# The last expert group's results: scattered to their tokens tile by tile instead of fetched by gathers

## The chip, the cores and the metric

The kernel runs on one core of a Trainium2 chip. The metric is the device time of one execution in microseconds (us); the kernel before takes 1362.29 us (median of three runs, 1362.22 to 1365.09).

## The reference

A "macaron" block over 4 sequences of 512 tokens with 128 features, all in float32. The input passes six residual stages; only the last one, a mixture of experts (MoE), is touched by the change:

```python
x = x + 0.5 * _L0_ffn_ref(_layernorm(x), ...)
x = x + _L0_attn_ref(_layernorm(x), ...)          # a state-space (mamba) scan
x = x + 0.5 * _L0_ffn_ref(_layernorm(x), ...)
x = x + 0.5 * _L1_ffn_ref(_layernorm(x), ...)     # MoE
x = x + _L1_attn_ref(_layernorm(x), ...)
x = x + 0.5 * _L1_ffn_ref(_layernorm(x), ...)     # MoE, the same weights
```

```python
rw = _route(x, gate_w, gate_bias)     # per token 8 of 64 experts, with weights; 0 elsewhere
expert_out = vmap(lambda gw, uw, dw: silu(x @ gw.T) * (x @ uw.T) @ dw.T)(Wg, Wu, Wd)   # 64 experts, 88 wide
routed = einsum('eth,te->th', expert_out, rw)
out = routed + shared                 # shared: one dense expert, 176 wide
```

The kernel computes for each token only its 8 chosen experts.

## The kernel before, in words

The engines are PE (TensorE), DVE (VectorE), ACT (ScalarE), POOL (GpSimd) and SP, which only issues DMAs. POOL issues the indirect DMAs, 128 rows each.

**The planner.** The program records every operation, with the tiles it reads and writes, into a `Plan`. `schedule` then orders each engine's queue by a model of costs (`costs`), data dependencies, free buffers and a rank (`rank(...)` sets one for each engine), and `issue` emits the operations in that order. Each engine works through its queue strictly in order. Line 558 is the call in `issue` that emits most operations, so most rows of the profile have that line and are told apart by their tiles. An `Op` with an `apart` name is a write to rows that no other write of that name touches, so that these writes do not wait for each other; `past` makes an operation wait for all writes of a name. Between two such writes POOL does a small memset (`scratch`, line 627).

**The MoE layer.** It runs twice. Each time the four sequences form two groups of two sequences (`GROUPS`), so there are four groups, g = 0 to 3; `LAST` in the changed kernel is g = 3. A group has 1024 tokens with 8 experts each, that is 8192 rows.

- `send` (line 1065) routes one sequence and works out for each token and each of its 8 experts the row in the DRAM tensor `sent` that this pair gets. Rows of one expert are contiguous and padded to whole tiles of 128 rows. `at` holds the row numbers as integers and `top` as floats, both with one added before and taken off after. `xt` is the normalized input, token by token (128 partitions, 4 tiles of tokens). 32 scatters per sequence (4 tiles x 8 experts, `scatter`, line 1147) write the rows.
- `by_tiles` (line 1165) runs the experts on 96 tiles (`OFTEN`), in 24 batches of four tiles. `batch` (line 1170) loads four tiles with one DMA (`xr`, three buffers), transposes them on PE (`xc`), multiplies with the expert's gate and up weights, applies silu and the product (`hr`), transposes (`hc`) and multiplies with the down weights; ACT copies the result out of PSUM (`yr`) and SP writes it to the DRAM tensor `back`, in the same row order as `sent`. A row is addressed as partition times 128 (`most`) plus the tile's number. PE reads the number of each tile's expert into registers. If a group needs more than 96 tiles, a branch (`rest`, line 1248) does the others; every engine passes that branch, and on the path that skips it the queue waits for its DMAs. `nothing` and `zero` clear `sent` and part of `back` at the start (`clear`), so that padded rows hold zeros.
- `take` (line 1291) fetches the results of one sequence: for each tile of 128 tokens 8 gathers (`gather`, line 1156, on POOL, from `back` by `at`) into tiles `y` (16 buffers), and DVE adds them up with the routing weights `by` into `total` (one product and seven `scalar_tensor_tensor`). In the second layer each tile of tokens is then transposed on PE, added to x on DVE and written to the output by SP.

**The order at the end.** `work` (line 1454) is `by_tiles` and then `take` for both sequences. A group is worked on after the next one has been sent. So POOL's queue ends with: the sends of g = 3, the 64 gathers of g = 2 (after the branch of g = 2, beside the experts of g = 3), and the 64 gathers of g = 3 (after the branch of g = 3).

Of the kernel before, what the change touches and what calls it, by code (L numbers as in the profile page):

```python
# [24 lines left out]
F32 = mybir.dt.float32  # L27
U32 = mybir.dt.uint32
I32 = mybir.dt.int32
AF = mybir.ActivationFunctionType  # L30
ALU = mybir.AluOpType
AX = mybir.AxisListType
PSUM = bass.MemoryType.PSUM

P = 128
NB, S, D = 4, 512, 128
NT = S // P
# [14 lines left out]
MOST = {n: ((n * S * TOPK + E * (P - 1)) // P + 3) // 4 * 4 for n in (1, 2)}  # L52
OFTEN = {2: 96, 1: 72}
INDIRECT = 1.25
READ = 4
PART = 11

# [221 lines left out]
class Plan:  # L279
# [100 lines left out]
    def costs(self, op):  # L380
# [36 lines left out]
        if op.name in ("scatter", "gather"):  # L417
            return INDIRECT, INDIRECT + 6.0
        if op.eng == "gpsimd":
# [153 lines left out]
def macaron(ctx: ExitStack, tc: tile.TileContext, a: dict, out: bass.AP):  # L573
# [50 lines left out]
    numbers = fixed.tile([P, 1], F32, tag="numbers", name="numbers")  # L624
    real.gpsimd.iota(numbers, pattern=[[0, 1]], base=0, channel_multiplier=1, allow_small_or_imprecise_dtypes=True)
    scratch = fixed.tile([1, 8], F32, tag="scratch", name="scratch")
    plan.between = lambda: real.gpsimd.memset(scratch, 0.0)
# [41 lines left out]
    most = MOST[2]  # L669
    sent, backs = ([dram.tile([most * P, D], f"{n}{i}", bufs=1) for i in range(k)] for n, k in (("sent", 3), ("back", 2)))  # L670
    rank(0, 0, 0, 15)
    nothing = stage.tile([P, 2 * D], "nothing", bufs=1)
    nc.gpsimd.memset(nothing, 0.0)
    zero = dram.tile([P * 8 * D], "zero", bufs=1)
    for i in range(4):
        nc.sync.dma_start(out=zero.rearrange("(p x) -> p x", p=P)[:, i * 2 * D : (i + 1) * 2 * D], in_=nothing)
    chunks = []
    for rows in sent:
        to = rows.rearrange("(n p i) d -> n p (i d)", n=most // 8, i=16)
        chunks += [(to[n], zero.rearrange("(p x) -> p x", x=16 * D)) for n in range(most // 8)]  # L680
    for rows in backs:
        to = rows.rearrange("(p i) d -> p (i d)", p=P)
        for i in range(min(OFTEN.values()), most, 8):
            chunks.append((to[:, i * D : (i + 8) * D], zero.rearrange("(p x) -> p x", p=P)))
    chunks = iter(chunks)
# [350 lines left out]
    def count(b, prior):  # L1036
# [19 lines left out]

        xt = slots.tile([P, NT, D], "xt", bufs=2, fifo=True)
        ps = aux()
        plan.hold(xt)
        for t in range(NT):  # L1060
            nc.tensor.transpose(ps[:, t * P : (t + 1) * P], xn[:, t * P : (t + 1) * P], ident)
        nc.scalar.copy(xt.rearrange("p t d -> p (t d)"), ps)
        return xn, m8, sc, ranks, xt

    def send(g, b, before_):
# [4 lines left out]
        with plan.turn("route"):  # L1070
# [42 lines left out]
            for t in range(NT):  # L1113
                nc.vector.max(top[:, t, :], at_row[:, t, :])
                nc.vector.tensor_scalar_add(at[:, t], top[:, t], -1.0)

            with ranked(0.6, 5.7 if g < 2 and b else 1.6, 1, 5, g):
# [8 lines left out]
        for t in range(NT):  # L1126
            for k in range(TOPK):
                scatter(rows, at[:, t, k : k + 1], xt[:, t], g)
        return dict(ranks=ranks, held=held, base=base, end=end, mine=mine, taken=taken, fetch=(at, by), xn=xn, rows=rows)
# [16 lines left out]

    def scatter(rows, at, x, g):
        def go():
            return real.gpsimd.indirect_dma_start(  # L1149
                out=rows.real(), out_offset=bass.IndirectOffsetOnAxis(ap=at.real(), axis=0),  # L1150
                in_=x.real(), in_offset=None,
            )

        plan.call("gpsimd", "scatter", go, [rows], [at, x], f"sent{g}")

# [9 lines left out]
    def by_tiles(g, rows, of, taken, tiles, often):  # L1165

        back = backs[g % 2]
        firsts, lasts = firsts_of, lasts_of.rearrange("p e d -> p (e d)")

        def batch(nc, tiles_of, first, x, bank, xt, hs, ht, y, product, experts_, hold):  # L1170
            some = slice(first, first + 4)
            loads = nc.sync.dma_start(out=x, in_=tiles_of(rows)[:, some])
            experts_()
            ps = bank()
            hold(xt)
            for j in range(4):
                nc.tensor.transpose(ps[:, j * P : (j + 1) * P], x[:, j], ident)
            nc.vector.tensor_copy(xt, ps)
            for j in range(0, 4, 2):
                ps = bank()  # L1180
# [19 lines left out]
            nc.scalar.copy(y.rearrange("p i d -> p (i d)"), ps)  # L1200
            nc.sync.dma_start(out=tiles_of(back)[:, some], in_=y)
            return loads

        def tiles_of(x):
            return x.rearrange("(p i) d -> p i d", p=P)

        def buffers():
            return (
                bpool.tile([P, 4, D], "xr", bufs=3, fifo=True),
                bpool.tile([P, 4 * P], "xc", fifo=True),  # L1210
                bpool.tile([P, 4, I], "hr", fifo=True),
                bpool.tile([P, 4 * P], "hc", fifo=True)[0:I],
                bpool.tile([P, 4, D], "yr", fifo=True),
            )

# [10 lines left out]
        for first in range(0, often, 4):  # L1226
# [3 lines left out]
            def product(ps, lhs, w, n, j, to=to, held=held):  # L1230
# [6 lines left out]

            x, *others = buffers()
            batch(
                nc, tiles_of, first, x, lambda: banks.tile([P, S], "bank"), *others, product,  # L1240
                lambda: plan.call("tensor", "registers", partial(read, to, first), [held], [of]), plan.hold,
            ).past = f"sent{g}"


        x, *others = buffers()
        bank = banks.tile([P, S], "bank")

        def rest(past):
# [3 lines left out]
            )  # L1252
            x_, bank_, rows_, back_, *others_ = (v.real() for v in (x, bank, rows, back, *others))
            with tc.If(needed > often, preferred_fallthrough_block=False, name="rest"):
                for first in range(often, tiles, 4):
                    to = {}

                    def product(ps, lhs, w, n, j, to=to):
# [4 lines left out]
                    load = batch(  # L1263
                        real, lambda v: tiles_of({rows: rows_, back: back_}[v]), first, x_, lambda: bank_, *others_,
                        product, lambda: read(to, first), lambda *_: None,
                    )
                    past(load)

        plan.hold(x, bank, *others)
        plan.call("tensor", "branch", rest, [back], [rows, of, taken, firsts, lasts]).past = f"sent{g}"  # L1270
# [19 lines left out]

    def take(b, back, at, by, to=None):

        total = tpool.tile([P, NT, D], "total", bufs=1, fifo=True)
        for t in range(NT):
            y = [tpool.tile([P, D], "y", bufs=2 * TOPK, fifo=True) for _ in range(TOPK)]
            for k in range(TOPK):
                gather(y[k], back, at[:, t, k : k + 1])
            nc.vector.tensor_scalar_mul(total[:, t], y[0], by[:, t, 0:1])
# [155 lines left out]
    def work(g, blocks, rows, of, taken, fetch):  # L1454
        rank(12 + g if g < len(GROUPS[0]) else 19 + g, 2, 2, 6 + g, g)
        back = by_tiles(g, rows, of, taken, MOST[len(blocks)], OFTEN[len(blocks)])
        for b, f in zip(blocks, fetch):
            rank(0.4, 1.5, 1.5, 6, g + 0.5)
            take(b, back, *f, to=out[:, b * S : (b + 1) * S] if g >= len(GROUPS[0]) else None)

# [92 lines left out]
```

## Time and profile before

| | us |
|---|---|
| median of three runs | 1362.29 |
| the profiled execution | 1361.67 |
| its span, first to last instruction | 1359.9 |
| PE busy | 1151.3 (85%) |
| DVE busy | 983.2 (72%) |
| ACT busy | 638.9 (47%) |
| POOL busy | 557.0 (41%) |
| 256 scatters of `sent` on POOL | 282.2, 1.102 each |
| 256 gathers of `y` on POOL | 245.8, 0.960 each |
| scatters of g = 3, second sequence | from 1116.48 to 1158.18 |
| last copy of g = 2's results on ACT | 1163.34 |
| gathers of g = 2 | from 1168.94 to 1249.85 |
| last copy of g = 3's results on ACT | 1267.53 |
| gathers of g = 3 | from 1272.18 to 1351.80 |
| last addition to x on DVE | 1354.29 |

The profile is of one execution. A group of instructions is written as line, engine, operation, out<-in, with count, busy time and mean duration, then the idle time of that engine just before them and what ended it. "issue" means that the engine waited for nothing that the profile shows. In tables by stage the columns are the stretch (from:to and length), then for each engine its busy time and its number of instructions, then the clock granted to TensorE, the share of time that the DMA engines were busy, and GB/s. In the timeline a line is start, duration, engine, line, operation, and in brackets the idle time before it with what ended it. The chain that ended last is a list of start, duration and what the time went to.

### The profile page before, as it was taken

The page shows a single profiled execution, that of the slowest core. Times are in us where ns is not written, and L with a number is a line of the kernel's source. Part 1 is how long each engine was busy: PE and PEld are TensorE (multiplying, and loading weights), DVE is VectorE, ACT ScalarE, POOL GpSimd, SP SyncE. Part 2 cuts the span into 40 slices and gives each one's busy share as a digit, 9 for nine tenths or more (in the row PEclk, how much of TensorE's full clock was granted, in tenths as well). Part 3 has the DMA queues.
Part 4 walks back from the last instruction along what each step waited for, and adds up shares of the span by engine and source line. Part 5 has one row for each costly group of instructions (what it writes and reads, how often), then busy time and mean ns, then how long its engine had stood idle before and what let it go on. Part 6 is the DMA issues. An engine that isn't in the chain of part 4 may idle for free. (4 is left out here: it accounts for less than half of the span.)

```text
span 1359.9 us, 17468 instructions
## 1 busy us (share of the span) xinstructions
PE 1151.3 (85%) x5006; PEld 704.2 (52%) x5006; DVE 983.2 (72%) x2425; ACT 638.9 (47%) x1207; POOL 557.0 (41%) x794
## 2 busy tenths in 40 slices
PE   6999998999999978999789979999899889778200
PEld 4853332333343423579688645555556669778200
DVE  2168798999999895779477568988869688476222
ACT  4775866687755335343235535435353544222100
POOL 0000000000018593556677177380816418575475
PEclk8999998999999988999899989999999999898655
DMA  5074794755512208346466111010111136565221
GB/s 172 23 266 155 264 282 131 227 154 178 133 36 68 59 28 277 107 155 199 159 200 177 53 54 53 24 51 3 53 34 59 59 107 204 166 196 152 78 60 49
DMA packets 76313, 166.74 MB, mean 123 GB/s; under 512 B 17880, under 2 KB 30193, under 8 KB 75089
## 3 DMA queue, kind: packets, MB, share of 16 engines
q1 hardware_dynamic: 59825, 131.89, 30.9%
q0 software_dynamic: 16384, 33.59, 8.2%
q8 instruction: 50, 0.82, 0.2%
q14 instruction: 54, 0.44, 0.1%
HBM read 117.44 MB, written 83.36 MB: 148 GB/s over the span
## 5 line engine op out<-in xcount | busy, mean ns | idle before, releaser
L1149 POOL DMA_INDIRECT sent<-xt,at x256 | 282.2, 1102 | 171.3 <-issue 62.9
L1158 POOL DMA_INDIRECT y<-back,at x256 | 245.8, 960 | 147.2 <-issue 34.7
L558 PE MATMUL bank<-h,h 128*128 128x512 f32 (+1 forms) x576 | 242.4, 563 | 8.1 <-DVE h L558 6.4
L558 PEld LDWEIGHTS bank<-h,h 128*128 128x128 f32 x576 | 108.0, 194 | 127.7 <-issue 111.7
L1232 PE MATMUL bank<-gate_up,xc 128*128 x768 | 152.1, 324 | 3.8 <-DVE xc L558 3.4
L558 ACT ACTIVATE hr<-bank 128x176 f32<-128x176 f32 x192 | 60.0, 318 | 155.1 <-PE bank L1232 152.1
L558 DVE TENSOR_TENSOR_SCAN hs<-da,hs 128x512 f32<-128x512 f32 (+1 forms) x128 | 132.1, 1074 | 0.2
L1232 PEld LDWEIGHTS bank<-gate_up,xc 128*128 128x128 f32 x768 | 122.4, 196 | 15.1 <-issue 7.2
L558 DVE SCALAR_TENSOR_TENSOR total<-y,by,total 128x128 f32<-128x128 f32 x224 | 77.9, 348 | 69.7 <-DMA y<-back,at 68.4
L1232 PE MATMUL bank<-down,hc 88*128 x768 | 125.3, 280 | 1.7 <-DVE hc L558 1.1
L558 ACT ACTIVATE h<-bank,vec 128x512 f32<-128x512 f32 (+1 forms) x108 | 67.2, 639 | 113.1 <-PE bank L558 112.4
L1232 PEld LDWEIGHTS bank<-down,hc 88*128 88x128 f32 x768 | 112.4, 195 | 5.1 <-DVE hc L558 1.4
L558 ACT ACTIVATE p<-p,a_low 128x256 f32<-128x256 f32 (+3 forms) x128 | 70.8, 554 | 88.3 <-DVE a_low L558 88.1
L558 POOL MEMSET eq<- 128x256 f32 x8 | 2.6, 324 | 240.8 <-DVE gt L558 223.0
L558 ACT ACTIVATE da<-rep,neg_a 128x512 f32<-128x512 f32 (+1 forms) x160 | 88.7, 625 | 26.5 <-DVE hs L558 24.9
L558 PE MATMUL bank<-ident,xr 128*128 128x128 f32 x384 | 82.6, 283 | 17.8 <-DMA xr<-sent 17.8
L558 POOL MEMSET xn<- 128x3 f32 x4 | 0.4, 98 | 234.7 <-PE bank L558 234.7
L558 DVE COPY xc<-bank 128x512 f32<-128x512 f32 x96 | 65.7, 685 | 41.0 <-PE bank L558 40.5
L558 PE MATMUL bank<-kt,q 128*128 128x512 f32 (+3 forms) x256 | 85.7, 457 | 10.9 <-DVE q L558 8.7
L558 PE MATMUL bank<-ident,total 128*128 128x128 f32 x32 | 9.3, 341 | 100.4 <-DVE total L558 100.1
L558 ACT COPY yr<-bank 128x512 f32<-128x512 f32 x96 | 56.1, 587 | 71.6 <-PE bank L1232 66.1
L558 ACT ACT_TABLE_LOAD x69 | 88.5, 1283 | 2.0 <-PEq L1546 0.8
(188 smaller groups left out, 2154.9 us busy)
## 6 DMA issues: line engine op xcount, KB each, us to landing
sent<-zero SPq DMA_DIRECT2D x48, 512.0 KB
xr<-sent SPq DMA_DIRECT2D x96, 256.0 KB
back<-yr SPq DMA_DIRECT2D x96, 256.0 KB
rep<-spread SPq DMA_DIRECT2D x48, 256.0 KB
back<-zero SPq DMA_DIRECT2D x14, 512.0 KB
bc<-kept SPq DMA_DIRECT2D x24, 256.0 KB
rep<-spread SPq DMA_DIRECT2D x32, 128.0 KB
sent<-xt,at POOLq DMA_INDIRECT x256
```

The lines of the kernel that those rows point to most:

```text
L558: ins = getattr(getattr(self.nc, op.eng), op.name)(*(real(x) for x in op.args), **{k: real(x) for k, x in op.kw.items()})
L1149: return real.gpsimd.indirect_dma_start(out=rows.real(), out_offset=bass.IndirectOffsetOnAxis(ap=at.real(), axis=0), in_=x.real(), in_offs ...
L1158: return real.gpsimd.indirect_dma_start(out=y.real(), out_offset=None, in_=rows.real(), in_offset=bass.IndirectOffsetOnAxis(ap=at.real(), ...
L1232: return real.tensor.matmul(ps.real(), lhsT=lhs.real(), rhs=w.real()[..., bass.ds(to["at"][j] * n, n)], start=True, stop=True)
```

## The change

For the last group (g = 3) the results are no longer written in the order of `sent` and gathered. Each batch scatters its four tiles to a DRAM tensor `home`, in which the 8 results of one token lie next to each other; the results of a tile of tokens are then read with two plain DMAs on SP.

For that each sent row carries its way home. A row of `sent` becomes W = 144 floats: 128 features, 8 floats with the 8 row numbers of the token (plus a mark of the group), and 8 floats with the target row less the row number. In a batch DVE compares the 8 row numbers of each row with the number of the slot it lies in (`slot`), multiplies the match with the other 8 floats and sums, which gives the target row `to`; rows that match nothing (padding) get a target of their own behind the first `HOME` rows. This takes five small DVE instructions per batch. All four groups send the wider rows; only the last one uses them.

`y` of the last group takes the buffers of two attention tiles (`p3` and `q`, two each), the loads from `home` the room of `vo` (eight parts of 4 results). The buffers of gathered rows go from 16 to 12. The planner is told that a home scatter ends 2 us after its issue (other indirect DMAs: 6 us). The diff, cut to its core:

```diff
+LAST = sum(map(len, GROUPS)) - 1
+W = D + 2 * TOPK
+HOME = 2 * S * TOPK
+MARK = 32768.0
...
         if op.name in ("scatter", "gather"):
-            return INDIRECT, INDIRECT + 6.0
+            return INDIRECT, INDIRECT + (2.0 if op.apart == "home" else 6.0)
...
+    slot = fixed.tile([P, MOST[2]], F32, tag="slot", name="slot")
+    real.gpsimd.iota(
+        slot, pattern=[[1, MOST[2]]], base=0, channel_multiplier=MOST[2], allow_small_or_imprecise_dtypes=True
+    )
+    goal = fixed.tile([P, 2 * NT, TOPK], F32, tag="goal", name="goal")
+    real.gpsimd.iota(
+        goal, pattern=[[P * TOPK, 2 * NT], [1, TOPK]], base=1 - HOME, channel_multiplier=TOPK,
+        allow_small_or_imprecise_dtypes=True,
+    )
...
+    sent = [dram.tile([most * P, W], f"sent{i}", bufs=1) for i in range(3)]
+    backs = [dram.tile([most * P, D], f"back{i}", bufs=1) for i in range(2)]
+    home = dram.tile([HOME + most * P, D], "home", bufs=1)
...
-        xt = slots.tile([P, NT, D], "xt", bufs=2, fifo=True)
+        xt = slots.tile([P, NT, W], "xt", bufs=2, fifo=True)
...
-        nc.scalar.copy(xt.rearrange("p t d -> p (t d)"), ps)
+        nc.scalar.copy(xt[:, :, 0:D], ps.rearrange("p (t d) -> p t d", t=NT))
...
+            n = 1 if before_ else 0
+            nc.vector.tensor_scalar_add(xt[:, :, D : D + TOPK], top, (g + 1) * MARK - 1.0)
+            nc.vector.tensor_tensor(xt[:, :, D + TOPK :], goal[:, n * NT : (n + 1) * NT], top, ALU.subtract)
...
-        back = backs[g % 2]
+        last = g == LAST
+        back = home if last else backs[g % 2]
...
-                nc.tensor.transpose(ps[:, j * P : (j + 1) * P], x[:, j], ident)
+                nc.tensor.transpose(ps[:, j * P : (j + 1) * P], x[:, j, 0:D], ident)
             nc.vector.tensor_copy(xt, ps)
+            if last:
+                own, mine, to = where
+                wide = [P, 4, TOPK]
+                nc.vector.tensor_scalar_add(own, x[:, :, D : D + TOPK], -(g + 1) * MARK)
+                nc.vector.tensor_tensor(own, own, slot[:, some].unsqueeze(2).to_broadcast(wide), ALU.is_equal)
+                nc.vector.tensor_mul(own, own, x[:, :, D + TOPK :])
+                nc.vector.tensor_reduce(mine, own, AX.X, ALU.add)
+                nc.vector.scalar_tensor_tensor(to, mine, float(HOME), slot[:, some], ALU.add, ALU.add)
...
-            nc.sync.dma_start(out=tiles_of(back)[:, some], in_=y)
+            if last:
+                for j in range(4):
+                    send_back(to[:, j : j + 1], y[:, j])
+            else:
+                nc.sync.dma_start(out=back.rearrange("(p i) d -> p i d", p=P)[:, some], in_=y)
...
+            y = apool.tile([P, S], ("p3", "q")[next(buffer) % 2], fifo=True).rearrange("p (i d) -> p i d", i=4)
+            own, mine, to = (tpool.tile([P, 4, n], m, dtype=t) for n, m, t in ((TOPK, "own", F32), (1, "mine", F32), (1, "to", I32)))
...
+                lambda at, y: scatter(home, at, y, "home"),
...
-            y = [tpool.tile([P, D], "y", bufs=2 * TOPK, fifo=True) for _ in range(TOPK)]
-            for k in range(TOPK):
-                gather(y[k], back, at[:, t, k : k + 1])
+            y = []
+            if room is None:
+                for k in range(TOPK):
+                    y.append(tpool.tile([P, D], "y", bufs=12, fifo=True))
+                    gather(y[k], back, at[:, t, k : k + 1])
+            else:
+                of = back[0:HOME].rearrange("(m p k) d -> m p (k d)", p=P, k=TOPK)[n * NT + t]
+                for i in range(2):
+                    part = room[:, (2 * (n * NT + t) + i) % 8]
+                    nc.sync.dma_start(
+                        out=part.rearrange("p k d -> p (k d)"), in_=of[:, i * 4 * D : (i + 1) * 4 * D]
+                    ).past = "home"
+                    y += [part[:, k] for k in range(TOPK // 2)]
...
+        room = None
+        if g == LAST:
+            room = apool.tile([P, NT, HEADS, D], "vo", bufs=1).rearrange("p t (i k) d -> p (t i) k d", i=2)
```

## The prediction

> **What bounds the kernel now.** I read the page first: engines by slice, and the costliest groups.
>
> ```profile
> POOL 0000000000018593556677177380816418575475
> L1149 POOL DMA_INDIRECT sent<-xt,at x256 | 282.2, 1102 | 171.3 <-issue 62.9
> L1158 POOL DMA_INDIRECT y<-back,at x256 | 245.8, 960 | 147.2 <-issue 34.7
> ```
>
> POOL works in bursts of indirect DMAs, and each costs POOL about a microsecond however little it moves. Next the stages at the end: the last group's experts, then its fetch.
>
> ```profile
> core 0: us, PE busy (x) PEld busy (x) DVE busy (x) ACT busy (x) POOL busy (x), PEclk, DMA share, GB/s
> 1169.00:1250.00 81.00, 67.84 (x462) 64.89 (x463) 54.43 (x147) 21.98 (x56) 61.66 (x64) 0.88 0.62 185
> 1250.00:1272.00 22.00, 15.50 (x124) 14.92 (x123) 9.81 (x22) 7.23 (x16) 0.00 (x0) 0.97 0.31 112
> 1272.00:1360.00 88.00, 3.60 (x8) 1.46 (x8) 23.82 (x72) 0.00 (x0) 60.43 (x64) 0.50 0.19 54
> ```
>
> In the last 88 us nothing but POOL is busy, and DVE only now and then. That is what the change aims at. But in the first row POOL is nearly full too: beside the last group's experts it fetches the group before (64 gathers). Its free time there is the 22 us of the middle row. POOL's timeline gives the pace:
>
> ```profile
> 1155.95 0.96 POOL L1149 DMA_INDIRECT sent<-xt,at  x1 [0.21 <-DVE hr L558]
> ...
> 1157.22 0.97 POOL L1149 DMA_INDIRECT sent<-xt,at  x1 [0.21 <-issue]
> 1168.94 0.97 POOL L1158 DMA_INDIRECT y<-back,at  x1 [10.74 <-SPq L1254]
> ...
> 1248.91 0.94 POOL L1158 DMA_INDIRECT y<-back,at  x1 [0.30 <-issue]
> 1272.18 0.94 POOL L1158 DMA_INDIRECT y<-back,at  x1 [22.32 <-SPq L1254]
> ...
> 1350.86 0.94 POOL L1158 DMA_INDIRECT y<-back,at  x1 [0.30 <-issue]
> ```
>
> A quiet scatter takes 1.27 us (1155.95 to 1157.22, a 0.09 us memset included), a gather (1350.86 - 1272.18) / 63 = 1.249 us alone and (1248.91 - 1168.94) / 63 = 1.269 us beside the experts. The chain that ended last closes with:
>
> ```profile
> 1350.86 2.42 DMA y<-back,at
> ...
> 1353.37 0.36 DVE total L558
> ...
> 1353.78 0.49 PE bank L558
> 1354.29 0.29 DVE x L558
> ```
>
> A gather lands 2.4 us after its issue, the sum follows it at once; 1354.58 to the span's end, 5.3 us, is the last write of out. From the last gather's issue to the end: 1359.9 - 1350.86 = 9.0 us.
>
> **The change part by part.** The sum is made on the profiled execution, 1361.67 us with a span of 1359.9 (1.8 us outside); the median of the runs is 0.6 us above it.
>
> *Removed:* 64 gathers of the last group (1272.18 to 1350.86 plus landing), and its 24 writes of back by SP (0.32 us of SP each, beside other work: nothing).
>
> *Added on POOL, the term that decides:* 96 scatters, one for each of the 96 tiles (24 batches of four; tiles are padded, so 96 and not 64). In the built program POOL's queue holds all 64 gathers of the third group ahead of the first of them, so they can't use the time before 1249.85 (1248.91 + 0.94). The first begins 0.30 later (gap 0.21, memset 0.09) at 1250.15, though batches have been finished since 1182. Pace: the floor is the quiet 1.27; the other end is the scatters at 480 to 496 us, beside two-input DVE work without a break:
>
> ```profile
> 486.81 1.20 DVE L558 TENSOR_TENSOR hs<-rep,bc 128x1024 f32<-128x1024 f32 x1
> 486.86 1.99 POOL L1149 DMA_INDIRECT sent<-xt,at  x1 [0.21 <-issue]
> ```
>
> There one takes 2.25 us (484.65 to 486.86 to 489.15). The last stage is nearest to the expert stage, where a gather lost 0.02 us to the neighbours (1.269 against 1.249): I take 1.29. The last scatter is issued at 1250.15 + 95 x 1.29 = 1372.7; by the floor 1370.8.
>
> The section "1. Specifications" of the Trainium skill's GPSIMD Engine Reference says that GpSimd's SBUF interfaces are shared with VectorE, and that DVE instructions in a 2-port mode or with two SBUF inputs contend with it; the rows at 486 us agree (1.99 against 0.96). Read strictly, it speaks against this change: each batch brings three such DVE instructions beside the scatters, and if each held POOL for all of its time the end would be some 13 us later, near 1426.
>
> *Waits added.* The copy of a batch's result (ACT) now waits for the scatters of four batches before (two tags, two buffers each), the target rows "to" (DVE, two buffers) for those of two batches before. Behind "to" on DVE stand the later batches' hr, xc and hc; POOL would starve if it came late. A batch's scatters take 4 x 1.29 = 5.2 us. If a scatter lands like a gather, 1.5 us after its issue has ended, "to" is ready about 1.7 us into the next batch's 5.2, and DVE has 2 x 0.33 + 0.69 + 0.68 + 5 x 0.19 = 3.0 us of work per batch. PE needs about 4 us per batch (96 us for 24 in the trace). So POOL is what all wait for, and I cost these waits at nothing; the cover is gone if landing takes over 4.5 us.
>
> *Added on DVE:* five small instructions per batch (0.19 us, the row of a 128x32 TENSOR_TENSOR): 23 us in all, under POOL's 123. Two more per send, eight sends: at most 3 us, under the attention and expert work of PE; zero taken.
>
> *The new tail.* SP's loads of home wait for all scatters. In the trace the branch after the last write of back took from 1268.14 (issue) to 1271.23 (the chain's start): 3.1 us for landing and branch, taken for the last scatter too (bounds 2.4, a gather's landing, and 4.4, the same step at 1164.27 to 1168.68). Then SP's issue, 0.4; the first load 2.7 us (xr issued 1168.68, PE begins 1171.38). The loads are 16 of 256 KB, 4.2 MB: 19 to 23 us at the 222 GB/s of the first stage (75 to 240 us) or the 185 of the row above. DVE needs more: 56 dependent sums at 0.385 us (two back to back took 0.77), 8 products at 0.29, 8 additions to x at 0.29: 26.2 us. In before these lay under the gathers' pace; now they lie bare. Then 0.6 for PE and gaps, 5.3 for the write of out. From the last scatter's issue to the end: 3.1 + 0.4 + 2.7 + 26.2 + 0.6 + 5.3 = 38.3 us, for 9.0 before.
>
> *Ahead of it:* rows of 576 bytes for 512 (zeroing 48 chunks, 256 sends, 96 loads of 288 KB). One send is one POOL instruction of the same 128 rows: nothing. Zeroing grows by 3.1 MB; the waits between 60 and 260 us name no DMA that a compute engine waited for: nothing. Loads of xr: PE waited for them three times in the whole trace, at group starts (17.8 us): 12% of that, 2 us at most. Gather buffers 12 for 16: the first is free 9.0 us after its issue (sum at 1177.89), 12 x 1.27 = 15 us are covered. The planner orders the first stages anew; PE idles 165 - 153.7 = 11 us between 75 and 240 us, so I bound this by 11 us either way and take nothing.
>
> *Sum:* (1372.7 - 1350.86) + (38.3 - 9.0) = 21.8 + 29.3 = 51 us. 1361.67 + 51 = 1413 us.
>
> **The rivals.**
>
> *A. POOL's queue sets the end (the forecast):* 1413 us, 1401 to 1424 with the bounds of the pace near its floor, the branch, and half of the reordering.
>
> *B. The scatters themselves are slowed, or starve on "to".* For: DVE's two-input instructions (the 2.25 us row). Against: 0.56 us of such work per 5.2, where the slow row had it all the time. If three of 0.19 per batch hold POOL fully: 24 x 0.56 = 13 us, 1426. If landing takes 6 us: 24 x 1.5 = 36 more, 1449.
>
> *C. It is faster: the scatters run beside the experts and the 80 us of fetching go.* Place: POOL between 1250 and 1272. This decides if the last scatter is issued before 1359.9 - 38.3 = 1321.6, that is at a pace of (1321.6 - 1250.15) / 95 = 0.75 us. A scatter alone keeps POOL busy for 0.96. If they kept up with the experts (last copy 1267.5) the span would end near 1268 + 5 + 38 = 1311, 1313 us in all. For: POOL's 22 us of idleness, and that spans on POOL are rough in such a trace. Against: POOL's order and pace; 64 + 96 indirect DMAs from 1169 on are 204 us, for 160 us before with the idle 22.
>
> *D. The first 1169 us move more than what is added at the end.* Only by the reordering, 11 us at most by PE's idle time in that stage: 1402 or 1424 with A.
>
> **How the numbers follow.** A 72%, B 14%, D 10% (within A's signs, all slower), C 4%. The prediction is A's. The range takes A with D and B's lower half: 1400 to 1432; left out are C, B's starving case and a larger reordering, about 2 in 10. About 0.2% (2.7 us) is what a measurement of this kernel can tell from no change; almost no case ends there. Faster 4%, same 1%, slower 95%.
>
> **What would show it.** Right: 96 scatters in an unbroken row on POOL from about 1250 to 1373 at about 1.29 us, the chain of waits running through them, PE mostly idle beside them; then a tail of 16 loads with DVE busy for 26 us and the end 38 us after the last scatter. Wrong: scatters between the gathers; gaps on POOL that end at DVE's "to" or ACT's copy (B); a tail that waits for DMA and not DVE; the third group's first gather far from 1169 us (D).

## The result, and the profile after

The changed kernel takes 1417.22 us (median of four runs, 1414.65 to 1418.64) where the kernel before takes 1362.30: 1.0394 times as long (95% interval 1.0382 to 1.0407). The forecast was 1413 us in a range of 1400 to 1432. The profiled execution took 1416.43 us with a span of 1414.6.

The page of the changed kernel, POOL by slice (40 slices of 35.4 us) and the groups of indirect DMAs (L1169 are all scatters, L1178 the gathers):

```profile
POOL 0000000000066770827772574726354085778881
L1169 POOL DMA_INDIRECT sent<-xt,at x256 | 281.6, 1100 | 179.3 <-issue 113.2
L1178 POOL DMA_INDIRECT y<-back,at x192 | 183.8, 957 | 108.0 <-SPq L1299 35.1
```

64 gathers are gone, and POOL's late gap is gone too: it is busy from the third group's gathers to the next to last slice. The stages at the end, by engine:

```profile
core 0: us, PE busy (x) PEld busy (x) DVE busy (x) ACT busy (x) POOL busy (x), PEclk, DMA share, GB/s
1182.00:1261.90 79.90, 26.52 (x163) 23.36 (x163) 38.12 (x124) 7.32 (x20) 60.48 (x66) 0.63 0.31 91
1261.90:1385.00 123.10, 68.56 (x421) 60.77 (x421) 44.27 (x164) 21.65 (x52) 101.40 (x191) 0.79 0.27 89
1385.00:1414.60 29.60, 3.60 (x8) 1.45 (x8) 20.01 (x72) 0.00 (x0) 0.00 (x0) 0.50 0.49 162
```

Where the kernel before had PE work through the last group's experts beside the gathers (67.84 us of PE in 81), PE now does 26.52 of its us there and must leave 68.56 for the row of scatters: with four buffers for results, only the first batches can be worked out before POOL begins to empty them. The timeline of POOL and the tail:

```profile
1260.65 0.94 POOL L1178 DMA_INDIRECT y<-back,at  x1 [0.30 <-issue]
1261.58 0.09 POOL L642 MEMSET scratch<- 1x8 f32 x1
1261.90 1.01 POOL L1169 DMA_INDIRECT home<-p,to  x1 [0.22 <-issue]
...
1376.10 0.96 POOL L1169 DMA_INDIRECT home<-p,to  x1 [1.31 <-issue]
...
1383.71 0.96 POOL L1169 DMA_INDIRECT home<-q,to  x1 [0.21 <-issue]
...
1389.79 0.29 DVE L563 TENSOR_SCALAR total<-vo,by 128x128 f32<-128x128 f32 x1 [14.82 <-DMA vo<-home]
...
1401.55 3.23 DVE L563 SCALAR_TENSOR_TENSOR total<-vo,by,total 128x128 f32<-128x128 f32 x12
...
1410.83 0.47 PE L563 MATMUL bank<-ident,total 128*128 128x128 f32 x1 [2.19 <-DVE total L563]
1411.34 0.29 DVE L563 SCALAR_TENSOR_TENSOR x<-bank,x 128x128 f32<-128x128 f32 x1 [0.57 <-PE bank L563]
```

The first scatter follows the last gather directly. From it to the last there are 95 steps in 121.81 us, 1.282 us each; without the one late scatter (idle 1.31 before 1376.10, the second of its batch, so it waited neither for the batch's target rows nor for its result) the mean of the other 94 is 1.2705. Then 2.9 us until SP issues the first load (1386.61), 3.2 until it has landed, 21.0 us of DVE, 0.8 for the last tile's transpose and addition to x, and 3.0 us from that addition's end (1411.63) to the span's end.

Who waits beside the row of scatters, by the table of waits from 1262 to 1384 us (who <- for what: us in total, times, longest):

```profile
ACT p L563 <- DMA home<-p,to: 72.5, 6, 59.6
DVE to L563 <- DMA home<-p,to: 33.2, 11, 5.2
DVE to L563 <- DMA home<-q,to: 29.8, 11, 4.9
ACT q L563 <- DMA home<-q,to: 15.4, 6, 4.1
```

DVE and ACT wait for the landing of scatters, so that their buffers come free, and POOL does not wait for them: the target rows `to` were ready 2.6 us or more ahead of every batch's first scatter. Out of the chain that ended last (start, duration, what):

```profile
1358.48 0.97 POOL home L1169
...
1374.78 1.31 issue
...
1383.71 2.75 DMA home<-q,to
1386.61 3.15 DMA vo<-home
...
1391.66 1.61 DVE total L563 x6
```

POOL's scatters, their landing, the loads, the sums: it is the chain that the prediction laid out. The step it left at zero shows elsewhere: the third group's gathers begin at 1181.76 us and no longer at 1168.94.

### The profile page after: what moved, and what is told of

It is laid out like the page before. It is cut to its first block, busy times and chain, and to the rows that moved or that the text cites. A ratio compares the mean times of both kernels' runs of the same rounds, so it can differ in the third digit from the quotient of the medians.

```text
span 1414.6 us, 17711 instructions
## 1 busy us (share of the span) xinstructions
PE 1167.5 (83%) x5006; PEld 705.2 (50%) x5006; DVE 998.8 (71%) x2561; ACT 629.8 (45%) x1200; POOL 596.1 (42%) x924
## 3 DMA queue, kind: packets, MB, share of 16 engines
q1 hardware_dynamic: 58673, 136.15, 30.9%
## 5 line engine op out<-in xcount | busy, mean ns | idle before, releaser
L1169 POOL DMA_INDIRECT sent<-xt,at x256 | 281.6, 1100 | 179.3 <-issue 113.2
L1178 POOL DMA_INDIRECT y<-back,at x192 | 183.8, 957 | 108.0 <-SPq L1299 35.1
L1271 PE MATMUL bank<-down,hc 88*128 x768 | 122.0, 281 | 6.1 <-DVE hc L563 4.8
L563 ACT ACTIVATE p<-p,a_low 128x128 f32<-128x128 f32 (+3 forms) x128 | 70.8, 555 | 90.4 <-DVE a_low L563 90.1
L563 PE MATMUL bank<-ident,xr 128*128 128x128 f32 x384 | 85.5, 285 | 21.9 <-DMA xr<-sent 21.7
L563 ACT ACTIVATE da<-rep,neg_a 128x512 f32<-128x512 f32 (+1 forms) x160 | 88.8, 625 | 30.9 <-DVE hs L563 24.1
L563 PE MATMUL ys<-hs,sum 128*32 128x512 f32 (+1 forms) x320 | 75.0, 557 | 26.1 <-DVE hs L563 26.1
L563 PE MATMUL bank<-kt,q 128*128 128x512 f32 (+3 forms) x256 | 85.9, 458 | 12.2 <-DVE q L563 10.7
L563 PE MATMUL ys<-pt,vo 128*128 128x512 f32 (+3 forms) x256 | 82.4, 441 | 11.9 <-ACT pt L563 4.6
L563 DVE TENSOR_TENSOR hs<-rep,bc 128x1024 f32<-128x1024 f32 (+1 forms) x80 | 78.8, 994 | 17.9 <-PE ys L563 17.8
L563 DVE SCALAR_TENSOR_TENSOR total<-y,by,total 128x128 f32<-128x128 f32 x168 | 58.1, 347 | 45.1 <-DMA y<-back,at 44.1
```

The source lines that it names most:

```text
L563: ins = getattr(getattr(self.nc, op.eng), op.name)(*(real(x) for x in op.args), **{k: real(x) for k, x in op.kw.items()})
L1169: return real.gpsimd.indirect_dma_start(out=rows.real(), out_offset=bass.IndirectOffsetOnAxis(ap=at.real(), axis=0), in_=x.real(), in_offs ...
L1178: return real.gpsimd.indirect_dma_start(out=y.real(), out_offset=None, in_=rows.real(), in_offset=bass.IndirectOffsetOnAxis(ap=at.real(), ...
L1271: return real.tensor.matmul(ps.real(), lhsT=lhs.real(), rhs=w.real()[..., bass.ds(to["at"][j] * n, n)], start=True, stop=True)
```

## The experiments

**The chips.** The twelve runs fell on other chips (numbers 2, 5, 0 and 4), on which the kernel before takes 1637 to 1648 us. Up to 560 us the changed kernel's trace goes there as on the first chip (PE busy for 137.25 and 137.33 us between 400 and 560). Between 560 and 1100 us its granted clock is 0.85 in place of 0.98, and PE, DVE and ACT show pauses of several us together, which the profile mostly puts down to "remote", that is to nothing it records. So each ratio below is to the kernel before on the same chip, and what is compared in us is compared between runs on such chips. No trace of the kernel before was taken there.

The theories. P: POOL's queue sets the end, at about 1.28 us a scatter; its rivals are that the experts or the rows `to` hold the scatters back, and that two-input DVE work slows them (B of the prediction). D: the tail is DVE's; its rival is that the loads set it. O: the 12.8 us lost ahead of 1182 come from the order in which the planner issues the first stages; its rival R is that the wider rows cost them.

### The changed kernel on these chips

This run was made after eight of those told below, which it is the measure for.

> The changed kernel itself, on the chips of the experiments. Eight runs so far fell on two chips on which the kernel before takes 1639 to 1648 us: from 600 us on their granted clock is 0.80 to 0.88 where the first chip showed 0.94 to 1.00. Theory O (the order ahead of the last group costs about 0.8% there too, as the kernel before in the new order showed with 1.006 and 1.008): the ratio to the kernel before is 1.0278 + 0.008 = 1.036, and against it the fifth scatter adds 1.0501 - 1.036 = 1.4% (23 us, where POOL alone would add 31), and scattering first takes off 1.6% (26 us). If the order has no part in it there: 1.028, as with the old order. On a chip like the first: 1.039, 1417 us.

Measured: 1691.25 us for 1636.78, 1.0324 (1.0290 to 1.0358): 54.5 us more, where the first chip showed 54.9. Its row of scatters takes from 1501.16 to 1658.34, 157.2 us and not 122: POOL stands in 11 places, for 35 us together. The longest stand, with lines of ACT and DVE from the same trace:

```profile
1449.47 0.58 ACT L563 COPY q<-bank 128x512 f32<-128x512 f32 x1
...
1516.33 0.97 POOL L1169 DMA_INDIRECT home<-p,to  x1 [0.17 <-issue]
...
1523.74 0.53 ACT L563 ACTIVATE hr<-bank 128x176 f32<-128x176 f32 x2 [15.20 <-remote]
1524.59 0.16 DVE L563 SCALAR_TENSOR_TENSOR to<-mine,slot 128x4 int32<-128x4 f32 x1
1525.49 0.99 POOL L1169 DMA_INDIRECT home<-q,to  x1 [6.53 <-ACT q L563]
```

The profile names ACT's copy into `q`, but the copy that this fourth batch scatters is the one of 1449.47, done 75 us before. What came last are the batch's target rows `to`: ACT had paused for 15.2 us, DVE went on only after it, `to` was done at 1524.75, and the scatter began 0.74 us later. So it is in nine of the 11 places: each lies ahead of a batch's first scatter, which begins 0.74 or 0.75 us after the end of its `to`, with its copy done at least 7 us before. This is the starving on `to` of the prediction's rival B. Between such gaps the median step is 1.27 us, as on the first chip. The tail is 30.96 us, against 30.9 there.

### Does POOL's row set the end: a fifth scatter

```diff
+    aside = dram.tile([HOME + most * P, D], "aside", bufs=1)
...
                 for j in range(4):
                     send_back(to[:, j : j + 1], y[:, j])
+                if send_aside:
+                    send_aside(to[:, 0:1], y[:, 0])
...
+                lambda at, y: scatter(aside, at, y, "aside"),
```

> The changed kernel with a fifth scatter in each of the last group's 24 batches: the first tile once more, into a buffer in HBM that nobody reads. Theory P (POOL's row of scatters sets the end, 1.282 us each): 24 x 1.282 = 30.8 us more, 1448 us where the changed kernel takes 1417 and 30.8 us more than it anywhere. Rival (the scatters wait for what feeds them, the experts or the rows 'to', so that POOL has room in each batch): less than 10 us more. If the scatters are slowed by the DMA engines' traffic, more than 31 us.

Measured: 1721.91 us, 1.0501 (1.0469 to 1.0534), that is 1.77% of 1637, or 29 us, more than the changed kernel (on another chip of the kind); between the medians it is 30.7. POOL's row in the trace:

```profile
1544.31 0.96 POOL L1170 DMA_INDIRECT aside<-q,to  x1 [0.21 <-issue]
...
1545.58 0.96 POOL L1170 DMA_INDIRECT home<-p,to  x1 [0.22 <-issue]
...
1546.85 0.96 POOL L1170 DMA_INDIRECT home<-p,to  x1 [0.22 <-issue]
```

The steps stay at 1.27 us, and the row of 120 takes from 1510.14 to 1695.80, 185.7 us for 157.2: 28.5 us more for 24 scatters. The waits that come on top (35 us in the changed kernel, 34 here) neither grow nor are filled; why a longer row does not fill them no run shows. So theory P holds with its price, even on a chip on which the rows `to` hold POOL back now and then. The rival's "less than 10 us" is out; the 23 us of e9's expectation rested on a ratio of 1.036 for the changed kernel, which measured 1.0324.

### Do DVE's two-input instructions slow the scatters

```diff
                 nc.vector.tensor_tensor(own, own, slot[:, some].unsqueeze(2).to_broadcast(wide), ALU.is_equal)
+                for _ in range(6):
+                    nc.vector.tensor_tensor(own, own, own, ALU.mult)
                 nc.vector.tensor_mul(own, own, x[:, :, D + TOPK :])
```

> The changed kernel with six more two-input DVE instructions of 128x32 (0.19 us each, both inputs in SBUF; own times own, which leaves its values) in each of the last group's 24 batches. Three such instructions per batch are in the changed kernel. Theory P (POOL's pace hardly feels small two-input work): the step from one scatter to the next within an unbroken row stays at 1.28 us, 1.30 at most, and the time grows by less than 8 us, by the DVE work where that lies bare. Rival B (each such instruction holds POOL for all of its time): four scatters take 6 x 0.19 = 1.1 us more, 1.28 to 1.56 us a step, and where POOL sets the end the time grows by 24 x 1.1 = 27 us.

Measured: 1692.93 us, 1.0355 (1.0314 to 1.0396), with an interval that takes in the changed kernel's 1.0324; 1.7 us between the medians. What decides is the step from scatter to scatter, taken from the timeline without the gaps (steps under 1.6 us): 1.275 us in the mean of 79 steps, median 1.270, where the changed kernel shows 1.2875 in 84 on the same chip (median 1.270) and 1.2705 in 94 on the first. The steps left out could hide a slowing, but the whole row, gaps and all, takes 156.3 us here and 157.2 in the changed kernel, where the rival asks for 27 more. The new instructions by tile between 1500 and 1657 us (18 of the 24 batches; those of six lie ahead of the row), and a scatter beside three of them:

```profile
L563 DVE TENSOR_TENSOR own<-own x108: 176/191/263, 1507.0 to 1632.6; 128x32 f32<-128x32 f32 x108
```

```profile
1562.23 0.97 POOL L1169 DMA_INDIRECT home<-q,to  x1 [2.63 <-ACT q L563]
...
1562.71 0.64 DVE L563 TENSOR_TENSOR own<-own 128x32 f32<-128x32 f32 x3
...
1563.50 0.96 POOL L1169 DMA_INDIRECT home<-q,to  x1 [0.21 <-issue]
```

The scatter at 1562.23 has three two-input instructions within its 1.27 us and takes no longer. The rival's 1.28 to 1.56 us a step is out: two-input instructions of 128x32 did not hold the scatters.

### What POOL's order is worth: the scatters first

```diff
-        rank(12 + g if g < len(GROUPS[0]) else 19 + g, 2, 2, 6 + g, g)
+        rank(12 + g if g < len(GROUPS[0]) else 19 + g, 2, 2, 6 + g, g - 0.6 if g == LAST else g)
...
-        total = tpool.tile([P, NT, D], "total", bufs=1, fifo=True)
+        if room is None:
+            total = tpool.tile([P, NT, D], "total", bufs=1, fifo=True)
+        else:
+            total = apool.tile([P, S], "kt", bufs=1).rearrange("p (t d) -> p t d", t=NT)
```

The last number of `rank` is that of POOL's queue. In the program this puts 10 of the third group's gathers ahead of the 96 scatters, and 54 behind the last group's branch.

> The changed kernel with POOL's queue planned otherwise: the last group's 96 scatters stand behind only some ten of the third group's 64 gathers instead of behind all, and the other 54 gathers come after the last group's branch. Nothing is added; the sums of the last group get a buffer of their own. Theory P (POOL's queue sets the end, and what follows the last scatter lies bare only because nothing else is left): 1181.8 + 10 x 1.25 to the first scatter, 96 x 1.28 to the last, 4 for the branch, 54 x 1.25 of gathers with the loads of home and their sums beside them, 9 from the last gather: a span of 1397 us, 1399 us, 18 us under the changed kernel. Rival (POOL was not what the end waited for, or the experts' pace of about 4 us a batch holds the earlier scatters back): no gain, 1415 to 1420 us.

Measured: 1671.89 us, 1.0200 (1.0169 to 1.0232), 1.24% or 20 us less than the changed kernel (19.4 between the medians; expected 18). The timeline of POOL at the seam, and the end of the trace:

```profile
1590.47 0.96 POOL L1169 DMA_INDIRECT home<-q,to  x1 [0.21 <-issue]
1591.74 0.97 POOL L1178 DMA_INDIRECT y<-back,at  x1 [0.30 <-issue]
...
1665.66 0.95 POOL L1178 DMA_INDIRECT y<-back,at  x1 [0.30 <-issue]
```

```profile
1668.22 0.35 DVE L563 SCALAR_TENSOR_TENSOR total<-y,by,total 128x128 f32<-128x128 f32 x1 [0.84 <-DMA y<-back,at]
```

The loads of `home` and their sums now run beside the gathers, and the span ends 7.5 us after the last gather's issue instead of 31 after the last scatter's. The kernel stays slower than the one before: POOL still issues 160 indirect DMAs where that issues 128.

### What sets the tail: half the sums

```diff
-            for k in range(1, TOPK):
+            for k in range(1, TOPK // 2 if room is not None else TOPK):
```

> The changed kernel, whose last stage adds up only four of the eight results of each token (four of eight are left out of the sum; all are scattered and loaded). In the changed kernel's tail, from the issue of the last scatter to the span's end, 30.9 us, DVE is busy for 21 of them, with 8 products, 56 sums and 8 additions to x. Theory D (DVE sets the tail): 32 instructions of 0.28 us fall away, the tail is 30.9 - 9.0 = 22 us, and the time 9 us less. Rival (the 4.2 MB of loads set it): 28 to 31 us, since not a byte less is loaded.

Measured: 1685.59 us, 1.0269 (1.0213 to 1.0325), and a tail of 26.93 us from the last scatter's issue (1657.57) to the end: 4.0 us less than the changed kernel's, where D expected 9 and the rival 0 to 3. The chain of this run says why; this is one tile of its end:

```profile
1676.20 0.46 PE bank L563
1676.68 0.29 DVE x L563
1676.97 0.20 DVE total L563
1677.20 0.36 DVE total L563
1677.59 0.36 DVE total L563
1677.98 0.36 DVE total L563
1678.47 0.46 PE bank L563
```

No load stands in it, and in the table of waits from 1655 us on DVE waits for a load once, for the first:

```profile
DVE total L563 <- DMA vo<-home: 14.7, 1, 14.7
```

With less to add, the planner no longer lays the sums of two tiles into each other; each tile goes alone through one product, three sums that wait for each other (0.385 us from one start to the next), the transpose on PE and the addition to x: 2.28 us a tile, 8 x 2.28 = 18.2 us for 21.0. So DVE and its dependent steps set the tail, as D says, but the work per tile that is left is bound by its own chain and not by DVE's throughput. The rival is out; the size expected by D was wrong.

### What came ahead of the last group: order or width

Five kernels, in seven runs. The planner's `costs` for DMAs goes by bytes; the changed kernel's wider rows make some of them longer, and the planner then orders the first stages otherwise. One edit tells it the old lengths for those DMAs (or, in the kernel before, lengths 9/8 as long), and so gives each width nearly the other's order:

```diff
-        return max(0.1, size // run * 0.0095 + 0.05), 4 * size / 250e3
+        names = {x.tile.name for x in (*op.outs, *op.ins)}
+        told = size * D / W if names & {"xr", "nothing", "zero", "sent0", "sent1", "sent2"} and out.tile.name[:4] != "back" else size
+        return max(0.1, size // run * 0.0095 + 0.05), 4 * told / 250e3
```

The other edit leaves the scatters of the last group out and keeps the rest:

```diff
-LAST = sum(map(len, GROUPS)) - 1
+LAST = -1
```

> The changed kernel with its last group written back and fetched as before; the rows stay 576 bytes wide, with two more DVE instructions in each send and twelve gather buffers. What is left of the change lies ahead of the last stage. Theory O (the planner, which is told longer DMAs, issues the first stages in another order, and that costs about 12 us by 630 us): the third group's first gather near 1181 us instead of 1168.94, and the time 1362.3 + 12 = 1374 us. Theory R (the wider rows themselves, in bytes and in DVE work, cost the 12 us): 1374 us as well. If the 12 us came from the scatters of the last group or from what stands beside them, it would be 1362 us.

> The same wide rows, fetched as before, but the planner is told the old lengths for the DMAs of these rows and so issues nearly the order of the kernel before (21 of PE's 4764 instructions stand elsewhere, none of SP's). Theory O: the 12 us are gone, 1362 to 1365 us, the third group's first gather near 1169 to 1172 us. Theory R: the rows are as wide as in the run before, so 1374 us.

> The kernel before, with its 512-byte rows, but the planner is told lengths 9/8 as long for the DMAs of these rows, so that the first stages come in nearly the order of the changed kernel. Not a byte and not an instruction is added. Theory O: 1374 us, the third group's first gather near 1181 us. Theory R: 1362 us.

> The changed kernel, with the planner told the old lengths, so that all up to the last group comes in nearly the order of the kernel before. Theory O: the first scatter to home near 1250 us instead of 1261.9 and the time 1417.2 - 12 = 1405 us, within 3 us. Theory R: 1417 us.

> The changed kernel with the order of the kernel before ahead of the last group, a second time: the four runs above fell on a chip on which the kernel before itself takes 1648 us, its expert stages being slower, and there the order of the first stages could not show. Where the kernel before takes its 1362 us again, theory O (the order costs the 12 us): 1405 us within 3, the first scatter to home near 1250. Theory R (the wider rows do): 1417 us, as the changed kernel.

> The kernel before in nearly the order of the changed one, a second time. Where the kernel before takes 1362 us, theory O: 1374 us, within 3, and the third group's first gather near 1181 us. Theory R: 1362 us. With this run, the one above and the two kernels themselves every pairing of row width and order is measured.

> The changed kernel with both edits: the last group's scatters stand behind some ten of the third group's gathers, and the planner is told the old lengths, so that all ahead comes in nearly the order of the kernel before. If theory P and theory O hold apart from each other, their gains add: 1.0324 (the changed kernel) - 0.0124 (scattering first) - 0.0046 (old order) = 1.0154 times the kernel before, 1662 us where that takes 1637; on a chip where it takes 1362, 1417 - 18 - 12 = 1387 us. If the order's gain was chance, or lies in the same wait as the other: 1.020. In no case faster than the kernel before, since POOL still has 64 gathers and 96 scatters to issue where it had 128 gathers.

Measured, as ratios to the kernel before on the same chip:

| rows and last stage | old order | new order | new against old |
|---|---|---|---|
| narrow, gathered | 1 (the kernel before) | 1.0062 (1.0038 to 1.0086), 1.0082 (1.0051 to 1.0112) | +10 and +13 us |
| wide, gathered | 0.9932 (0.9908 to 0.9955) | 1.0009 (0.9991 to 1.0028) | +12 us |
| wide, scattered | 1.0272 (1.0247 to 1.0298), 1.0285 (1.0247 to 1.0323) | 1.0324 (1.0290 to 1.0358) | +9 and +6 us, intervals overlap |
| wide, scattered first | 1.0170 (1.0128 to 1.0212) | 1.0200 (1.0169 to 1.0232) | +5 us, intervals overlap |

Three things follow. The order costs: where not a byte and not an instruction changed, it took 10 and 13 us, and 12 with wide rows; in the changed kernel the difference has the same sign, but is not settled. The width does not cost on these chips: in either order the wide rows (with their 12 gather buffers and two DVE instructions more per send) are 8 to 11 us faster than the narrow ones, which neither theory expected, and whose cause stays open. So R falls on these chips; on the first chip order and width were never taken apart. But both together give 1.0009, and not the 1.009 that O expected of the first of these runs: here the two cancel, while the first chip shows 12.8 us lost.

The order can be seen in a stage that goes alike on all chips, 400 to 560 us. Of the kernel before, of wide rows in the old order (e2), of narrow rows in the new order (e3), and of the changed kernel:

```profile
400.00:560.00 160.00, 143.55 (x371) 57.63 (x370) 130.80 (x290) 68.28 (x91) 100.05 (x135) 0.93 0.32 100
```

```profile
400.00:560.00 160.00, 142.97 (x366) 57.30 (x365) 129.05 (x293) 67.94 (x90) 96.64 (x130) 0.91 0.32 103
```

```profile
400.00:560.00 160.00, 137.92 (x357) 53.09 (x356) 133.57 (x270) 67.23 (x90) 102.82 (x127) 0.91 0.32 98
```

```profile
400.00:560.00 160.00, 137.33 (x349) 52.06 (x348) 130.85 (x252) 66.89 (x90) 98.34 (x128) 0.89 0.32 103
```

The first number behind the length is PE's busy time. It goes by the order (143.55 and 142.97 in the old, 137.92 and 137.33 in the new) and not by the width. It is not a loss of 5 to 6 us, though: in the new order PE had done more before. On the first chip it was busy for 160.10 us between 75 and 240 with the change and for 153.67 before it, and over all 560 us it is only 2.4 us behind (510.7 against 513.1). The 12.8 us appear after that, as the first scatters of the first layer's third sequence show, before and after the change:

```profile
556.94 0.97 POOL L1149 DMA_INDIRECT sent<-xt,at  x1 [12.67 <-DVE same L558]
```

```profile
564.56 0.96 POOL L1169 DMA_INDIRECT sent<-xt,at  x1 [12.08 <-DVE same L563]
```

The second sequence's scatters had begun 3.7 us earlier than before the change (463.91 for 467.58); the third's begin 7.6 us later, the fourth's 12.2 (628.88 for 616.64), and from there the lag stays between 9 and 13. On the other chips the third begins at 558.02 with narrow rows in the new order (e3) and at 560.77 with wide rows in the old (e2), so that the lag does not show there, and then the pauses cover the stretch. That the order costs is measured; by what wait it costs, no run shows.

With both edits the changed kernel comes to 1.0170, between the 1.0154 expected of two separate gains and the 1.020 of one; it cannot be told. It is the best version of the change that was tried, and slower than the kernel before. The only kernel below 1 is the one with wide rows in the old order that gathers as before (0.9932): it scatters nothing home.

The part that scatters is the loss on these chips: with everything else of the change in place the kernel takes 1.0009, and with the scatters 1.0324, about 52 us more. On the first chip 12.8 of the 54.9 us lie ahead of it.

## Why the prediction was right, and where it was not

The sign, the mechanism and the size were right: 51 us forecast, 54.8 in the profiled executions (1416.43 - 1361.67). That the total came so close is in part luck, since two of its terms were off by more, against each other. By its terms, in us:

| term of the sum | forecast | measured |
|---|---|---|
| first scatter of the last group | 1250.15 | 1261.90 |
| 95 steps to the last | 122.6 (1.29 each) | 121.8 (1.282) |
| landing, branch and SP's issue | 3.5 | 2.9 |
| first load | 2.7 | 3.2 |
| DVE's products, sums, additions | 26.2 | 21.0, the last addition aside |
| PE, gaps (measured with the last addition) | 0.6 | 0.8 |
| last write of out to the end | 5.3 | 3.0 |
| end of the span | 1411.0 | 1414.6 |

- *POOL's pace* was right, and was what decided. It was reasoned from the expert stage, where a gather lost 0.02 us to its neighbours; the scatters kept the quiet 1.27 (1.2705 in the mean of 94), and the one late scatter makes it 1.282. The strict reading of the Trainium skill's GPSIMD Engine Reference, section "1. Specifications", by which each two-input DVE instruction would hold GpSimd, would have given 1426. The trace does not bear that out for 128x32 instructions of 0.19 us: with nine of them in a batch the step stayed at 1.275. At 486 us of the kernel before, beside 128x1024 instructions without a break, the section and the trace agree. What lies between these sizes was not measured.
- *The order of POOL's queue* was right: all 64 gathers ahead, the scatters in one row behind them.
- *The added waits at nothing* was right on the first chip: `to` was ready 2.6 us or more ahead of each batch's first scatter, where the prediction's 1.7 us into the batch before makes 3.5. The place that it named for the danger, POOL starving on `to`, is where it happens on the chips with pauses: the rows of scatters lose 31 to 38 us there. The prediction's condition for it, a late landing, is not the one: in both traces of the changed kernel the scatters' packets end within 2.6 us of the issue. DVE comes to `to` late, in the longest case behind ACT's pause of 15.2 us.
- *"The first 1169 us": nothing taken, 11 us either way.* This step failed; it cost 12.8 us. What the prediction bounded by PE's idle time between 75 and 240 us was not lost there. PE was busier there than before (160.1 for 153.7), and the lag appears between the second and the fourth sequence's scatters, from 525 to 629 us. The runs show that the planner's new order alone can cost 10 to 13 us; the wider rows are not the cause on the chips where it could be tried. It is rival D's event, a little beyond its bound.
- *The tail, 38.3 us*, was the right place and too large: 30.9. The term that was mis-sized is DVE's 56 sums at 0.385 us. That is the step of two sums that wait for each other; the planner lays the sums of different tiles into each other, and they start 0.26 us apart (12 in 3.23 us). The run with half the sums shows the other case, with 0.385 again. The bounds of the branch don't start alike: 3.1 is counted from the start of SP's last issue, 4.4 from its end (4.7 from its start), which changes nothing in the sum. The end was taken as 5.3 us from the kernel before, where SP waited for PE's queue for 2.5 us after the last write, which it does for 0.5 after the change:

```profile
SPq L1549 <- PEq L1549: 3.0, 2, 2.5
```

```profile
SPq L1608 <- PEq L1608: 0.7, 2, 0.5
```

- *"PE mostly idle beside them"* was wrong, without a price: PE is busy for 68.56 us of the scatters' 123, since only four batches fit ahead of them.

The two errors in size go against each other: 11.7 us more ahead, 0.7 less in the row, 7.4 less in the tail, together 3.6. Rival C (faster) needed a pace of 0.75 us. The prediction set 204 us of POOL's DMAs against "160 us before with the idle 22"; the 160 are without it, 183 with it (1168.94 to 1351.80), so that the margin against C was smaller than it reads. Its place, POOL's 22 idle us, is real, but with the scatters drawn ahead the gain is only 20 us of the 55.

## What to carry to other kernels

Count the instructions of the engine that issues indirect DMAs before counting bytes: a scatter of 128 rows costs GpSimd 1.27 us here and a gather 1.25, so that replacing 64 gathers by 96 scatters loses unless the scatters fill time in which that engine stood still, and the queue's order decides whether they do. Where a planner orders the program, a change of its inputs (here the length of a DMA) reorders stages that the edit does not touch; compare the queues, and give that a term of its own, since here 10 to 13 us came from it with not an instruction changed. For a row of sums, take the step of dependent ones only where nothing else can be laid between.

## What was not expected of the hardware

The chips differ more than the kernels: the kernel before takes 1362 us on one and 1637 to 1648 on four others. The pauses of PE, DVE and ACT on those four are not spread evenly. From 560 us on, what PE loses lies mostly beside POOL's rows of indirect DMAs; this is the changed kernel (e9) beside the 32 scatters of one sequence and in the stretch behind them:

```profile
1099.00:1140.00 41.00, 16.39 (x62) 9.08 (x61) 17.93 (x57) 5.93 (x18) 34.20 (x63) 0.75 0.16 56
1140.00:1203.00 63.00, 59.19 (x226) 34.60 (x226) 43.34 (x160) 27.73 (x65) 0.80 (x3) 0.94 0.06 16
```

PE is busy for 16.39 of 41 us with POOL at work and for 59.19 of 63 without; on the first chip it is busy for 35.87 of 40 beside such scatters (964 to 1004 us). Before 560 us such DMAs go without those pauses on these chips too, so that POOL's work alone is not the cause; what is, no run shows. The last group's row of scatters, which waits for the rows `to`, lost 31 to 38 us in every run there that has one, whether it had 96 or 120 scatters.

That the loss by the change is nearly the same in us, 54.9 on the first chip and 54.5 on another, is a coincidence of unlike parts: 12.8 us ahead of the last group and about 42 behind on the first, nearly nothing ahead and about 52 behind on the others. The kernels with rows of 576 bytes were 8 to 11 us faster than those with 512 on the same chip; nothing in the runs says why.
